# A perceiver layer on one Trainium2 core: the order of the first key matmuls and the first projection, 3 transfers for 24, and a later start of the ternary sums

## Chip, cores, metric

The kernel runs on one core of one Trainium2 chip. The metric is the device time of one execution in microseconds, as the median of several runs.

## What is computed

Eight sequences of 64 tokens (x, 512 wide) pass three residual blocks; ctx_2048 holds 1601 context rows for each sequence.

```python
# 1: cross attention over the context and self attention, quantised projections
ln_out = _ln(_layernorm(x), ln_w, ln_b)
q  = _ln(fp8_linear(ln_out, wq));  k = _ln(fp8_linear(ln_out, wk));  v = fp8_linear(ln_out, wv)
core = _gqa(q, k, v)                              # 16 heads in 8 groups, 128 wide
qx = _ln(fp8_linear(ln_out, wqx))
kx, vx = split(einsum('bsi,oi->bso', ctx_2048, w_kv_x))
kx = _ln(kx)
xout = _gqa(qx, kx, vx)                           # 1601 context rows
x = x + einsum(div_clamp_fp8(cat(core, xout)), wproj) * scales
# 2: token attention with a mask from a pairwise two-layer net, top 6 of 64 keys
x = x + sparse_attention(_layernorm(x))
# 3: feed forward, weights made ternary with a threshold of 0.7 of their mean magnitude
w1_q, w2_q = absmean_quant(w1), absmean_quant(w2)
x = x + einsum(gelu(einsum(_layernorm(x), w1_q) + b1), w2_q) + b2
```

## The kernel before

**Engines.** PE multiplies, ACT and DVE and POOL work elementwise, SP issues all transfers, each engine in its own order. Matrices that need more than one matmul pass of precision are split into a high part (a cast) and a low part (the remainder), and three products are summed: high x high, high x low, low x high.

**Cross attention.** Work is cut into 16 pieces (`Cross`, 8 sequences x 2 halves of the heads), each with 13 blocks of 128 context rows (`TT`; the last has 65). The main loop (L1156) has 227 slots; slot g does the keys of block g of the row of 208 blocks, and later stages of earlier blocks:
- `key_weights` (L491): loads the key weights of one half in four blocks of rows (`ic`), takes the mean off, casts `wkhi` on ACT (L501) and, for the first half, makes `wklo` on POOL (L502).
- `keys` (L542): loads a block of context (`cTr`), casts `cThi` on ACT (L549), makes `cTlo` on POOL (L550), 12 matmuls into `kx` (L555): four with `cThi` and `wkhi`, four with `cThi` and `wklo`, four with `cTlo` and `wkhi`. Then the squares (`ksq`, L560), a sum (`kxv`, L562), a power on POOL (`rqk`, L173) and the normalised `kn` on DVE (L564).
- `keys_t` (L567), one slot later: PE transposes `kn`, ACT and DVE make `kthi` and `ktlo`. Two buffers of `kt`, each holding a chunk of two or three blocks.
- `scores` (L580), two slots after a chunk's last keys: matmuls of `qxhi`, `qxlo` with `kthi`, `ktlo` (L598), which free the `kt` buffer. `queries` (L535) makes `qxhi` and `qxlo` on POOL before the first of them. Exponentials, transposes of the probabilities, context rows (`context`, L653) and the weighted sum (`weigh`, L678) follow 17 slots after the keys.
- `last_context` (L724), once, in slot 13: the last of the 1601 rows of all sequences is split into high and low; three rows (high, high, low) for each sequence are stored to `codd` in DRAM and loaded by `context` of the last block (L663).

**Background work.** Streams of generators are advanced in each slot: `bgA` 1.55 steps a slot and 4 from slot 142 (projections, self attention, output projection, token attention), `bgC` (the last pieces' end), `bgB` 0.4 steps a slot (`ternary`, L935). Their instructions are emitted at a lower priority and behind the slot's `pin` on DVE, that is behind the multiplication that makes `kn` (L564), by `issue_after` (L1242). `ternary` does for each of two weights 16 steps of a 256 KB load (`tern`) and a sum of magnitudes (L943, DVE), then 16 steps of a load, two DVE operations (L956, L958) and a store. The feed forward at the end reads the result, after slot 214. `tern` and the pairwise part of the token attention (`attn`, L760) share four buffers (`r2k`).

**The first projection** (`projection("qx", ..., first)`, L293) makes the first piece's queries: one step of five DVE operations that round the normalised tokens to fp8 (`b1y`, `xq`, L306 to L308), then four blocks of 256 columns: two weight loads (`ut`), four scalings on ACT (L325), eight matmuls (`pj`, L336), row statistics, and a transpose (`tr`, L372). In slot 0 all of it is emitted (`bgA.pump(ALL)`, L1184), behind the keys of block 0. The other tokens are normalised by `norms` (`token_norm`, L280: its result goes to DRAM as `lnTd` and is loaded again at L304), from slot 2, and are projected by the same function.

The instructions of an engine are not in the order of emission: the program is ordered when it is built, from priorities and simulated times (L1319).

Of the kernel before, what the change touches and what calls it, by code (L numbers as in the profile page):

```python
# [11 lines left out]
F32 = mybir.dt.float32  # L12
# [10 lines left out]
H = 512  # L23
NIC = 4
# [20 lines left out]
FAR = 3  # L45
PACE = 1.55, 4
LATER = 142
TERNARY_PACE, TERNARY_AT = 0.4, 8
HELD = "held"


# [6 lines left out]
def tile_perceiver(ctx: ExitStack, tc: tile.TileContext, t: dict):  # L58
    nc = tc.nc
    V, A, GP, PE = nc.vector, nc.scalar, nc.gpsimd, nc.tensor  # L60
# [3 lines left out]
    NB = NTOK // S  # L64
# [12 lines left out]
    def nm(s):  # L77
        uid[0] += 1
        return f"{s}_{uid[0]}"
# [4 lines left out]
    def sm(tag, k=1, dt=F32, bufs=None):  # L84
        kw = {} if bufs is None else {"bufs": bufs}
        return small.tile([P, k], dt, tag=tag, name=nm(tag), **kw)
# [5 lines left out]
    def mainp(tag="m"):  # L92
        return pm.tile([P, 512], F32, tag="m", name=nm(tag))

    def kxp(tag="kx"):


        if lane["late"] is not None:
            return lane["late"]
        return accp(tag) if lane["wide"] else mainp(tag)  # L100
# [28 lines left out]
    def load(dst, src):  # L129
        nc.sync.dma_start(dst, src)  # L130
        return dst
# [4 lines left out]
    def v3(ap, g):  # L136
        return ap.rearrange("p (g k) -> p g k", g=g)
# [4 lines left out]
    class Late:  # L142
# [13 lines left out]
        ps = staticmethod(lambda tag="b": kxp())  # L156
# [13 lines left out]
    def rsqrt(v, n, k, tag):  # L170

        y = sm(tag, k)
        GP.tensor_tensor(y[:n], v, mhalf[:n, :k], ALU.pow)  # L173
        return y[:n]
# [86 lines left out]
    def dtile(shape, dt, tag):  # L261
        return dram.tile(shape, dt, tag=tag, name=tag)
# [9 lines left out]
    wpd = [dtile([P, 2, H], F32, f"wpd{c}") for c in range(32)]  # L272
    clod = [dtile([SC, H], F32, f"clod{b}") for b in range(NB)]

    codd = [dtile([3, H], F32, f"codd{b}") for b in range(NB)]
    w1t = dtile([NIC, P, DFF], BF16, "w1t")
    w2t = dtile([NFC, P, H], BF16, "w2t")

# [170 lines left out]
    def cat_tile(tag):  # L449
        return ph.tile([P, 8, P], F32R, tag=tag, name=nm(tag), bufs=1)  # L450
# [69 lines left out]
    class Cross:  # L520
# [21 lines left out]
        def keys(self, tt):  # L542

            t0, n = TT[tt]
            raw = mp.tile([P, NIC, P], F32, tag="raw", name=nm("cTr"), bufs=3)
            paced[0] = nc.sync.dma_start(raw[:, :, :n], t["ctxT"][self.b].rearrange("(c p) k -> p c k", p=P)[:, :, t0:t0 + n])
            chi = mp.tile([P, NIC, P], F32R, tag="cThi", name=nm("cThi"), bufs=2)
            clo = mp.tile([P, NIC, P], F32R, tag="cTlo", name=nm("cTlo"), bufs=2)
            A.copy(chi[:, :, :n], raw[:, :, :n])  # L549
            GP.tensor_tensor(clo[:, :, :n], raw[:, :, :n], chi[:, :, :n].bitcast(F32), ALU.subtract)  # L550
            ps = kxp()
            k = 0
            for st, mv in ((chi, self.wk[0]), (chi, self.wk[1]), (clo, self.wk[0])):
                for ic in range(NIC):
                    PE.matmul(ps[:n], lhsT=st[:, ic, :n], rhs=mv[:, ic, :], start=k == 0, stop=k == 11)  # L555
                    k += 1
            kn = mp.tile([P, 512], F32, tag="kn", name=nm("kn"), bufs=3)
            sq = ksq
            v = sm("kxv", HG)
            A.activation(sq[:n, :, :D], v3(ps[:n], HG), AF.Square, scale=1.0 / math.sqrt(D))  # L560
            A.copy(kn[:n], ps[:n])
            V.tensor_reduce(v[:n], sq[:n], AX.X, ALU.add)  # L562
            r = rsqrt(v[:n], n, HG, "rqk")
            pin[0] = V.tensor_tensor(v3(kn[:n], HG), v3(kn[:n], HG), r.unsqueeze(2).to_broadcast([n, HG, D]), ALU.mult)  # L564
            self.kn[tt] = kn
# [158 lines left out]
    def last_context():  # L724
        raw = load(mp.tile([P, 512], F32, tag="raw", name=nm("cr"), bufs=3)[:NB], t["ctx"][:, SC - 1, :])
        hi = mp.tile([P, 512], F32R, tag="chi", name=nm("chi"), bufs=2)
        lo = mp.tile([P, 512], F32R, tag="clo", name=nm("clo"), bufs=2)
        A.copy(hi[:NB], raw)
        V.tensor_tensor(lo[:NB], raw, hi[:NB].bitcast(F32), ALU.subtract)
        for b in range(NB):  # L730
            for r, x in enumerate((hi, hi, lo)):
                nc.sync.dma_start(codd[b][r:r + 1], x[b:b + 1].bitcast(F32))

    ac = {}

# [403 lines left out]
    def norms(js):  # L1139
        for j in js:  # L1140
            token_norm(j)
            yield

    NT = len(TT)
    work = [Cross(b, half) for half in range(2) for b in range(NB)]
# [10 lines left out]
    for g in range(NA + LAG + 3):  # L1156
        nA, kA = divmod(g, NT)
        if g < NA and kA == 0:
            h = work[nA].half
            if h not in wk:  # L1160
                wk[h] = key_weights(h)
            work[nA].wk = wk[h]
        if g == LAG - 1:
            lane["wide"] = False
        if g == NA + 3:
            lane["late"] = mainp("late")
        e = g - LAG + 1
        if 0 <= e < NA:
            nE, kE = divmod(e, NT)
            w = work[nE]  # L1170
            if kE == CHUNKS[-1][0]:
                w.last_probs()
            w.context(kE)
            w.probs_t(kE)
            ci = CHUNK_OF[kE]
            if ci + 1 < NCH:

                with tc.issue_after(w.pin.ins):
                    w.exps(ci + 1, *((0, 2) if kE == CHUNKS[ci][0] else (2, 4)))
        if g == LAG - 4:  # L1180
            last_context()
        if g < NA:
            work[nA].keys(kA)
        if g == 0:  # L1184
            bgA.pump(ALL)
        if g == 2:
            bgA.add(norms(rest), projection("qx", range(4), rest), projection("qx", range(4, 8), range(NJ)),
                    projection("q", range(8), range(NJ)), projection("k", range(4), range(NJ)), projection("v", range(4), range(NJ)))
            bgA.add(*[self_attn(j) for j in range(NJ)])
            bgA.add(attn_consts())  # L1190
        if g == TERNARY_AT:
            bgB.add(ternary("ffn_w1", w1t), ternary("ffn_w2", w2t))
        if 0 <= g - 2 < NA:
            nS, kS = divmod(g - 2, NT)
            ci = CHUNK_OF[kS]
            w = work[nS]
            if kS == CHUNKS[ci][-1]:
                if ci == 0:
                    w.queries()
                w.scores(ci)  # L1200
                if ci == NCH - 1:
                    w.maxima()
                    w.exps(0, 0, 2)
        if 0 <= g - 3 < NA and (g - 3) % NT == NT - 1:
            work[(g - 3) // NT].exps(0, 2, 4)
        e = g - LAG
        if 1 <= e and e % NT == 0 and e // NT <= len(work):
            work[e // NT - 1].values()
        if 2 <= e and (e - 1) % NT == 0 and (e - 1) // NT <= len(work):
            w = work[(e - 1) // NT - 1]  # L1210
            key = (w.b // 2, w.half)
            j, odd = divmod(w.b, 2)
            split = w.half and j >= NJ - SPLIT
            if not odd:
                bgA.clear_front()
                if w.half:
                    bgA.pump(ALL)
                catq[key] = cat_tile("catx")
            w.cat(catq[key])
            if key != (NJ - 1, 1):  # L1220
                if not w.half:
                    if odd:
                        bgA.front.append(proj_part(j, 16, catq[key]))
                elif split or odd:
                    on = (odd * S, S) if split else (0, P)
                    bgA.add(finish(j, 24, catq[key], *on))
            elif not odd:
                bgC.add(proj_weights(24), finish(NJ - 1, 24, catq[key], 0, S, True, Late()))
            else:
                bgA.add(finish(NJ - 1, 24, catq[key], S, S, True))  # L1230
        if 0 <= e < NA:
            nE, kE = divmod(e, NT)
            work[nE].weigh(kE)
            if kE == NT - 1:
                work[nE].weighed()
        if 0 <= g - 1 < NA:
            nT, kT = divmod(g - 1, NT)
            work[nT].keys_t(kT)
        for bg, q in ((bgA, PACE[g >= LATER]), (bgC, PACE[1]), (bgB, TERNARY_PACE if g < NA + FFN_AT else 0)):
            n = int((g + 1) * q) - int(g * q)  # L1240

            with tc.issue_after(pin[0].ins), tc.issue_after(paced[0].ins) if bg is bgB else nullcontext(), tc.high_priority( -100):  # L1242
                bg.pump(n)
        if g == NA + FFN_AT:
            bgB.pump(ALL)
            if NJ > 2:
                bgB.add(ffn(list(range(NJ - 2)), 0))
                bgB.step()
# [74 lines left out]
```

## Time and profile before

| | |
|---|---|
| three runs, us | 1980.34, 1996.92, 1990.99 |
| median | 1990.99 us |
| span of the profiled execution, first to last instruction | 1990.0 us |
| mean granted clock of PE | 0.991 |
| instructions | 32306 |
| transfers | 352.02 MB, 177 GB/s on average |

The execution that was profiled has no other time than its span; it lies 1.0 us below the median of the three. The profile gives busy times of each engine (PE: matmuls, PEld: weight loads, DVE, ACT, POOL), the same in 40 slices of the span, the clock that PE was granted in tenths of full speed, and how busy the 16 transfer engines were. The chain of work that ended last is followed back from the last instruction; its largest shares:

```profile
PE 83%; DMA 7%; DVE 5%; issue 2%; ACT 1%; POOL 1%; SPq 0%; POOLq 0%; ACTq 0%; DVEq 0%
```

### The profile page before, as it was taken

The numbers are of one execution on the slowest core, as the hardware profiler recorded it, in microseconds if no ns is written. First come the engines' busy times: TensorE is split into PE (matmuls) and PEld (weight loads), VectorE is DVE, ScalarE is ACT, GpSimd is POOL, SyncE is SP. The second block draws the span as 40 slices with busy tenths as digits, with TensorE's granted clock in tenths as the row PEclk, the third lists the DMA queues.
The fourth block names the chain that finished last, engine by engine and source line by source line (L and its number), as shares of the span: only waits on it lengthen the run. The fifth ranks groups of instructions, "written<-read, shape, count | busy, mean of one in ns | idle before, by whom it ended". The sixth has DMA issues, their size and how long they took to land.

```text
span 1990.0 us, 32306 instructions
## 1 busy us (share of the span) xinstructions
PE 1923.4 (97%) x10709; PEld 1593.6 (80%) x10709; DVE 1377.2 (69%) x3423; ACT 1215.9 (61%) x2724; POOL 634.1 (32%) x600
## 2 busy tenths in 40 slices
PE   7899999999999999999999999999999999999998
PEld 5678888888888887887888788888877787886776
DVE  7768688677678676776775665756577665655665
ACT  6576667666676566655664545555675566566554
POOL 6343334333333333223332323222233333220132
PEclk9899999999999999999999999999999999999999
DMA  6345545466455654557776667656745543564425
GB/s 199 115 140 164 160 143 162 142 209 211 132 171 157 216 160 122 186 172 265 236 265 225 200 199 257 200 188 204 269 136 162 172 157 94 156 209 139 142 65 178
DMA packets 296503, 352.02 MB, mean 177 GB/s; under 512 B 30336, under 2 KB 191232, under 8 KB 296336
## 3 DMA queue, kind: packets, MB, share of 16 engines
q1 hardware_dynamic: 296336, 349.97, 55.5%
q8 instruction: 84, 1.38, 0.3%
q14 instruction: 83, 0.68, 0.1%
HBM read 283.94 MB, written 65.68 MB: 176 GB/s over the span
## 4 chain that ended last, share of the span: by engine, by line
PE 83%; DMA 7%; DVE 5%; issue 2%; ACT 1%; POOL 1%; SPq 0%; POOLq 0%; ACTq 0%; DVEq 0%
PE kx L555 26%; PE acc L693 8%; PE acc L694 8%; PE acc L695 8%; PE s L598 6%; PE pj L340 4%; PE pt L630 4%; PE kx L219 4%; DMA ws<-wpd 3%; PE xo L714 3%; PE pp L431 2%; PE p L822 1%; DMA wv<-in_wkv 1%; PE tr L372 1%; PE y L1073 1%
## 5 line engine op out<-in xcount | busy, mean ns | idle before, releaser
L550 POOL TENSOR_TENSOR cTlo<-cTr,cThi 128x512 fp32r<-128x512 f32 (+1 forms) x208 | 274.4, 1320 | 891.2 <-PE kx L555 618.1
L694 PE MATMUL acc<-plo,chi 128*128 128x512 f32 x768 | 310.3, 405 | 0.4 <-DVE plo L641 0.4
L695 PE MATMUL acc<-phi,clo 128*128 128x512 f32 x768 | 303.8, 397 | 0.0
L562 DVE TENSOR_REDUCE kxv<-ksq 128x4 f32<-128x516 f32 (+1 forms) x208 | 142.9, 687 | 223.0 <-ACT ksq L560 222.8
L173 POOL TENSOR_TENSOR rqk<-kxv,mhalf 128x4 f32<-128x4 f32 (+1 forms) x208 | 217.8, 1047 | 127.1 <-DVE kxv L562 109.5
L693 PE MATMUL acc<-phi,chi 128*128 128x512 f32 x768 | 246.7, 402 | 1.7 <-ACT chi L670 1.0
L555 PE MATMUL kx<-wkhi,cThi 128*128 128x512 f32 (+1 forms) x832 | 240.8, 411 | 7.0 <-ACT wkhi L501 2.3
L549 ACT CAST cThi<-cTr 128x512 fp32r<-128x512 f32 (+1 forms) x208 | 125.9, 606 | 182.1 <-PE kx L555 84.1
L555 PE MATMUL kx<-wklo,cThi 128*128 128x512 f32 (+1 forms) x832 | 230.4, 397 | 0.0
L555 PE MATMUL kx<-wkhi,cTlo 128*128 128x512 f32 (+1 forms) x832 | 229.4, 395 | 0.0
L577 ACT ACTIVATE kthi<-kx,cols 128x512 fp32r<-128x512 f32 (+1 forms) x208 | 140.8, 677 | 137.2 <-PE kx L219 135.6
L670 ACT CAST chi<-cr 128x512 fp32r<-128x512 f32 x192 | 119.1, 620 | 141.7 <-PE acc L694 130.5
L618 ACT ACTIVATE S<-S,cnm 128x256 f32<-128x256 f32 (+1 forms) x384 | 197.1, 522 | 7.0 <-DVE cnm L613 6.8
L578 DVE SCALAR_TENSOR_TENSOR ktlo<-kx,cols,kthi 128x512 fp32r<-128x512 f32 (+1 forms) x208 | 150.9, 726 | 60.7 <-ACT kthi L577 59.9
L555 PEld LDWEIGHTS kx<-wklo,cThi 128*128 128x128 f32 (+1 forms) x832 | 155.0, 187 | 41.2 <-issue 1.6
L555 PEld LDWEIGHTS kx<-wkhi,cTlo 128*128 128x128 f32 (+1 forms) x832 | 154.3, 186 | 41.3 <-issue 3.2
L555 PEld LDWEIGHTS kx<-wkhi,cThi 128*128 128x128 f32 (+1 forms) x832 | 147.5, 188 | 39.2 <-ACT wkhi L501 3.5
L564 DVE TENSOR_TENSOR kn<-kn,rqk 128x512 f32<-128x512 f32 (+1 forms) x208 | 149.4, 718 | 39.4 <-POOL rqk L173 36.3
L602 DVE CUSTOM_DVE_ANT_0 S<-s,zeros 128x256 f32<-128x256 f32 (+1 forms) x384 | 151.9, 429 | 33.1 <-PE s L598 32.2
L694 PEld LDWEIGHTS acc<-plo,chi 128*128 128x128 f32 x768 | 145.0, 189 | 26.4 <-issue 1.7
L693 PEld LDWEIGHTS acc<-phi,chi 128*128 128x128 f32 x768 | 139.9, 189 | 32.7 <-ACT chi L670 2.8
L695 PEld LDWEIGHTS acc<-phi,clo 128*128 128x128 f32 x768 | 144.6, 189 | 26.1 <-issue 1.6
(344 smaller groups left out, 3770.5 us busy)
## 6 DMA issues: line engine op xcount, KB each, us to landing
cTr<-in_ctxT SPq DMA_DIRECT2D x192, 256.0 KB
cr<-in_ctx SPq DMA_DIRECT2D x192, 256.0 KB
ws<-wpd SPq DMA_DIRECT2D x88, 512.0 KB
clod<-clo SPq DMA_DIRECT2D x96, 256.0 KB
clo<-clod SPq DMA_DIRECT2D x96, 256.0 KB
wv<-in_wkv SPq DMA_DIRECT2D x64, 256.0 KB
tern<-in_ffn_w SPq DMA_DIRECT2D x64, 256.0 KB
wpd<-ws SPq DMA_DIRECT2D x32, 512.0 KB
```

The lines of the kernel that those rows point to most:

```text
L173: GP.tensor_tensor(y[:n], v, mhalf[:n, :k], ALU.pow)
L550: GP.tensor_tensor(clo[:, :, :n], raw[:, :, :n], chi[:, :, :n].bitcast(F32), ALU.subtract)
L555: PE.matmul(ps[:n], lhsT=st[:, ic, :n], rhs=mv[:, ic, :], start=k == 0, stop=k == 11)
L562: V.tensor_reduce(v[:n], sq[:n], AX.X, ALU.add)
L564: pin[0] = V.tensor_tensor(v3(kn[:n], HG), v3(kn[:n], HG), r.unsqueeze(2).to_broadcast([n, HG, D]), ALU.mult)
L577: A.activation(hi[:, :, o], v3(pt, HG)[:, :, :n], AF.Copy, scale=hw["kx"])
L578: V.scalar_tensor_tensor(lo[:, :, o], v3(pt, HG)[:, :, :n], hw["kx"], hi[:, :, o].bitcast(F32), ALU.mult, ALU.subtract)
L602: V.tensor_tensor_reduce(sc[:, g, :cw], ps[:, :cw], zeros.to_broadcast([P, cw]), 1.0, -3.0e38, ALU.add, ALU.max, self.mx[:, g * NCH + ci:g ...
L618: A.activation(self.S[ci][:, g, :cw], self.S[ci][:, g, :cw], AF.Exp, bias=self.nmx[:, g:g + 1], accum_out=self.su[:, g * NCH + ci:g * NCH ...
L693: PE.matmul(self.U[ic], lhsT=chi[:n, s], rhs=phi[:n], start=tt == 0, stop=False)
L694: PE.matmul(self.U[ic], lhsT=chi[:n, s], rhs=plo[:n], start=False, stop=False)
L695: PE.matmul(self.U[ic], lhsT=clo[:n, s], rhs=phi[:n], start=False, stop=False)
```

## The change

Four edits. (1) For the first block of keys alone, the 12 matmuls go by block of weight rows, with the three products of a block together. (2) The rest of the first projection is emitted in slot 1, behind the second keys, and no longer in slot 0; its first step comes with the background work at the end of slot 0. (3) `codd` is one DRAM tensor of three rows for each of eight sequences, written by three transfers. (4) The ternary stream starts in slot 30 instead of 8.

```diff
-TERNARY_PACE, TERNARY_AT = 0.4, 8
+TERNARY_PACE, TERNARY_AT = 0.4, 30
...
-    codd = [dtile([3, H], F32, f"codd{b}") for b in range(NB)]
+    codd = dtile([NB, 3, H], F32, "codd")
...
-            k = 0
-            for st, mv in ((chi, self.wk[0]), (chi, self.wk[1]), (clo, self.wk[0])):
-                for ic in range(NIC):
-                    PE.matmul(ps[:n], lhsT=st[:, ic, :n], rhs=mv[:, ic, :], start=k == 0, stop=k == 11)
-                    k += 1
+            order = [(st, mv, ic) for st, mv in ((chi, self.wk[0]), (chi, self.wk[1]), (clo, self.wk[0])) for ic in range(NIC)]
+            if tt == 0 and self is work[0]:
+                order = [(st, mv, ic) for ic in range(NIC) for st, mv in ((chi, self.wk[0]), (clo, self.wk[0]), (chi, self.wk[1]))]
+            for k, (st, mv, ic) in enumerate(order):
+                PE.matmul(ps[:n], lhsT=st[:, ic, :n], rhs=mv[:, ic, :], start=k == 0, stop=k == 11)
...
-        for b in range(NB):
-            for r, x in enumerate((hi, hi, lo)):
-                nc.sync.dma_start(codd[b][r:r + 1], x[b:b + 1].bitcast(F32))
+        for r, x in enumerate((hi, hi, lo)):
+            nc.sync.dma_start(codd[:, r, :], x[:NB].bitcast(F32))
...
-        if g == 0:
+        if g == 1:
             bgA.pump(ALL)
```

## The prediction

> **What bounds the kernel now.** I read the totals and the 40 slices of the page first, then the list of who made PE (TensorE) wait, then the timeline of the first 130 us.
>
> ```profile
> PE 1923.4 (97%) x10709; PEld 1593.6 (80%) x10709; DVE 1377.2 (69%) x3423; ACT 1215.9 (61%) x2724; POOL 634.1 (32%) x600
> PE   7899999999999999999999999999999999999998
> ```
>
> PE is busy for 1923.4 of 1990.0 us: all idle time is 66.6 us. Only the ends of the slice line fall below 9. An edit that removes no matmul can win only from these 66.6 us and from matmuls that run at half pace. PE's waits up to 130 us:
>
> ```profile
> PE tr L219 <- DVE fa L201: 10.8, 1, 10.8
> PE pj L340 <- ACT ws L325: 4.6, 1, 4.6
> PE pt L630 <- ACT S L618: 2.4, 1, 2.4
> PE kx L555 <- ACT wkhi L501: 2.3, 2, 1.9
> PE kx L555 <- ACT cThi L549: 2.1, 1, 2.1
> ```
>
> With four smaller ones (1.7, 1.6, 1.2, 1.0) this makes 27.7 us; 10.8 of it is before the first transpose, whose load and row norm the change leaves alone. So 16.9 us of early idle time are open to it. The timeline of PE in the start:
>
> ```profile
> 15.84 0.80 PE L555 MATMUL kx<-wkhi,cThi 128*128 128x512 f32 x1 [1.91 <-ACT wkhi L501]
> 16.43 1.91 PE L555 MATMUL kx<-wklo,cThi 128*128 128x512 f32 x4
> 18.14 1.91 PE L555 MATMUL kx<-wkhi,cTlo 128*128 128x512 f32 x4
> 19.93 8.14 PE L336 MATMUL pj<-ws,xq 128*128 128x256 f32 x32
> 29.06 1.08 PE L555 MATMUL kx<-wklo,cThi 128*128 128x512 f32 x4
> ```
>
> Four key matmuls follow one another every 0.43 us at 16.4 and every 0.23 us at 29. Counts per microsecond put the step at 21.8 us (3 projection matmuls a microsecond before it, 6 after). The granted-clock column reads 1.00 there; it does read 0.50 at 68 to 72 us, after the stall at 62.9 to 67.5, with the same 0.43 us pace.
>
> **First keys by blocks of rows.** 12 matmuls stay 12. The old order needs all four blocks of the high weights (wkhi) before any low one: PE stands 1.91 us for the fourth block (cast at 15.17 on ACT), and 8 of the 12 matmuls are still to come at 16.43. In the new order, blocks 0 to 2 can be done by then: the context's low part was ready at 13.57 (POOL L550, 11.85+1.72), wklo block 2 at 15.24 (13.53+1.71), block 3 at 17.25 (15.86+1.39). After block 3's two matmuls on wkhi the last one starts at 17.25 and is done by 17.7, against 20.0 now: 2.3 us earlier. Two ACT scalings of the projection's weights (0.91 us at 14.37) that stand before the fourth cast now lose their place, which may give another 0.7. But what fills the freed time runs at the slow pace until about 21.8, so 2.3 us of it hold 2.3 x 0.23/0.43 = 1.2 us of later work. Bounds 1.2 and 2.3+0.7 = 3.0; I take 2.0, between the paces.
> In the Trainium skill, "TensorE: Matmul & The Clock Gate", Part 1, says that the array runs at half rate until a window of about 3.4 us was busy. By that rule a denser start could release the clock a little earlier, and the gain would go towards 3 us, the sum below from 4.5 to 5.5; the row above (busy from 15.84, fast at 21.8) needed some 6 us and does not settle it.
>
> **First projection behind the second keys.** 32 matmuls, 8 weight loads, 16 ACT scalings, four DVE chains: the same instructions, later. Emitted now in slot 0 in whole, it will give its first step (five DVE operations that make xq) at the end of slot 0, at low priority and behind the normalisation kn of the first keys (L564, done at 23.24 now, about 21 then, as its matmuls end 2.3 earlier); the rest follows the second keys. The five operations took 14.52 to 19.88 = 5.4 us beside POOL's weight splitting; the same forms elsewhere take 0.69+0.28+0.28+0.28+0.42+0.68 = 2.6. So xq is there at 23.6 to 26.4 instead of 19.9. PE does not stand: the second keys' high part is ready at 17.9, the low part at 19.34, the third's at 21.45. SP's transfer for the second keys (issued at 11.20, behind four loads of the projection's weights) may go earlier. Behind it: the projection ends 4 to 6.5 us later, and its chain of four transposes and the split into qxhi and qxlo with it. The split ends at 42.32 now and the first scores start at 46.27: 3.95 us of cover. Beyond it, the next key transposes need the kt buffers that these scores free; PE has one more block of keys (2.8 us) to pull ahead. A shift of 6.5 us less 3.95 is 2.55, under 2.8. Cost 0 to 2.5; I take 0.5, as the cover is nearly always enough.
>
> **Ternary sums from slot 30.** The pace of 0.4 a slot puts 9 steps between slots 8 and 30; they move behind. Each is a 256 KB load (0.50 us of SP) and a reduction of 0.68 us on DVE: 6.1 us of DVE until 250 us (9 rows there). Nothing waited for these reductions. The loads do meet the critical chain at one place:
>
> ```profile
> 49.82 0.33 SPq L290 DMA_DIRECT2D lnTd<-fb  x1
> 52.22 0.33 SPq L130 DMA_DIRECT2D ld<-lnTd  x1
> ...
> 54.01 0.32 SPq L290 DMA_DIRECT2D lnTd<-fb  x1
> 57.01 0.32 SPq L130 DMA_DIRECT2D ld<-lnTd  x1
> ...
> 58.30 0.49 SPq L130 DMA_DIRECT2D tern<-in_ffn_w  x1
> 58.89 0.38 SPq L290 DMA_DIRECT2D lnTd<-fb  x1
> 63.35 0.33 SPq L130 DMA_DIRECT2D ld<-lnTd  x1
> 63.77 0.39 SPq L130 DMA_DIRECT2D ld<-in_wqx  x1
> ```
>
> From storing lnTd to the load back it takes 2.4 and 3.0 us, but 4.5 when a ternary load goes in just ahead. SP holds in_wqx behind it, ACT's scaling of that waits, and PE stands 4.6 us. Without the ternary load the weights come up to 4.5-3.0 = 1.5 to 2.1 us earlier; a shorter stall also shortens the slow stretch (12 key matmuls at 0.43 instead of 0.23 = 2.4 us). But DVE is full from 55 to 65 us, with nothing ternary in it, and sets xq anyway. Bounds 0 and 2.1+2.4 = 4.5; I take 2.0.
> The other end: 64 steps end near slot 189 instead of 167, from 1530 to about 1530 x 189/167 = 1730 us. The 9 steps that come there are splits, 0.57+0.74 = 1.3 us of DVE each, 12 us over 200 us in which DVE is idle for 74 (200 less 126 busy, 1550 to 1750). Cover holds: 0. The weights that they write are read after slot 214. They share four r2k buffers with the pairwise part of the token attention; a wait there costs PE at most what it idles now in that stretch, 2.6 us.
>
> **Odd context rows in 3 transfers.**
>
> ```profile
> L732 SPq DMA_DIRECT2D codd<-chi x16: 232/250/455, 76.9 to 92.1; - x16
> L732 SPq DMA_DIRECT2D codd<-clo x8: 215/250/251, 78.3 to 92.4; - x8
> ```
>
> 21 issues of 0.25 us less: 5.3 us of SP. Only the five between 90.99 and 92.66 stand right before a context load that PE wants, and PE stands 2.1 us at 96.3 to 98.4 for its cast. But on ACT that cast stands behind a copy that waits for PE's own transposes (until 96.8), so the load alone would not move it. Bounds 0 and 2.1; I take 1.0.
> [...]
>
> **Sum.** 2.0 - 0.5 + 2.0 + 1.0 = 4.5 us. 1990.0 - 4.5 = 1985.5 for the span; the median of the three runs (1980.34, 1996.92, 1990.99) is 1.0 above the span: 1986.5.
>
> **Rivals.**
> 1. *The late projection delays the first scores* (slower). It decides once they start after 46.27+2.8 = 49.1 us. If DVE takes the five operations late and PE does the third and fourth keys first, the projection starts at 30 instead of 19.9: scores at 46.27+10-3.95 = 52.3, a stall of 3.2 us and 2.4 us of half pace behind it, and the later norms, which end in the 4.6 us stall, slip by as much: 5.6+5.6 less the gains of 4.5 = +6.7: 1998. For it: xq is now tied to kn; against: PE waited only 1.5 us between 20 and 57.
> 2. *All of it is hidden*: the 62.9 to 67.5 stall is DVE's, and takes up whatever the start gained: 1991.
> 3. *The whole early stretch closes*: 16.9 us of idle and 5.5 of half pace: 1968.6. Every wait would have to go; they have eight different causes.
> 4. *The order changes elsewhere.* The program's order on each engine is made from simulated times (L1319), so a moved step can shuffle later slots. Between 130 and 1850 us PE idles only some 24 us; 20 more would make 2011. Nothing in the profile says which way.
>
> **How the numbers follow.** Forecast 0.53, rival 1 0.22, rival 2 0.13, rival 3 0.04, rival 4 0.08. Three runs scatter from -11 to +6 us about their median, and 1% (20 us) is about what a measurement can tell from no change. Range 1974 to 1999: the forecast less that scatter, up to rival 1. Faster by over 1% takes rival 3 and luck: 0.05. Slower: rival 4: 0.08. Within: 0.87.
>
> **What will show it.** First keys done near 17.7; second keys before the first projection matmul, which starts at 24 to 26; first scores by 47; no ternary row before 230 us; storing lnTd to loading it at 3 us or less; PE idle before 130 us near 23. A stall of over 3 us ahead of the first scores, or over 35 us of idle between 130 and 1850, would make the forecast wrong.

## The result and the profile after

The changed kernel takes 2008.84 us (median of 6 runs, 2006.23 to 2013.36) against 1990.12 us for the kernel before in the same comparison. The ratio is 1.0086 with a 95% interval of 1.0064 to 1.0108: it is slower, by some 17 us. The execution that was profiled took 2009.42 us; its span is 2007.7, so 1.7 us lie around the span.

The totals and PE's slices of the changed kernel's page:

```profile
PE 1931.3 (96%) x10709; PEld 1600.2 (80%) x10709; DVE 1369.9 (68%) x3423; ACT 1213.4 (60%) x2724; POOL 634.8 (32%) x600
PE   6899999999999998999999999999999999999998
```

The same 10709 matmuls keep PE busy for 7.9 us more (1931.3 against 1923.4: more of them at the low clock), and PE idles 9.8 us more (76.4 against 66.6). The first slice falls from 7 to 6. PE's longest waits up to 140 us, in the list of who waited for whom (total, times, longest):

```profile
PE tr L219 <- DVE fa L201: 10.8, 1, 10.8
PE pj L336 <- DVE xq L308: 5.9, 1, 5.9
PE pj L340 <- ACT ws L325: 5.3, 1, 5.3
PE kx L219 <- DVE kn L564: 2.6, 2, 2.4
```

The second line is new: the first projection waits 5.9 us for xq. The two waits that the edits were thought to shorten differ: the one for `wkhi` is gone, the one for the projection's weights (`ws`) is 5.3 instead of 4.6. The timeline of PE in the start:

```profile
18.05 0.50 PE L556 MATMUL kx<-wklo,cThi 128*128 128x512 f32 x1
18.39 1.09 PE L556 MATMUL kx<-wkhi,cThi 128*128 128x512 f32 x4
19.32 1.09 PE L556 MATMUL kx<-wklo,cThi 128*128 128x512 f32 x4
20.24 1.07 PE L556 MATMUL kx<-wkhi,cTlo 128*128 128x512 f32 x4
27.19 9.49 PE L336 MATMUL pj<-ws,xq 128*128 128x256 f32 x32 [5.88 <-DVE xq L308]
```

The first keys are through at 18.5 (20.0 before), and the second keys run at once, at the fast pace of 0.23 us: both are done at 21.3, where the kernel before had done the first and 1.4 us of the projection. Up to here the change leads. Then PE has nothing: its next instruction is the projection, and PE does not step past it to the third keys, which start at 37.1 although POOL has made the low parts of the third and the fourth block by 23.95. The same stretch in windows (length, PE busy and matmuls, granted clock, transfer share, GB/s):

```profile
23.50:27.00 3.50, 0.00 (x0) 0.73 0.89 256
27.00:31.60 4.60, 4.41 (x10) 0.50 0.05 19
31.60:36.50 4.90, 4.90 (x23) 0.97 0.00 2
```

During the wait the clock was taken down (0.73 on average from 23.5 to 27, so 0.50 from about 25.1), and the first 10 projection matmuls ran at 0.50. The 32 took 9.49 us against 8.14 before. The wait's cause is on DVE:

```profile
21.07 1.75 DVE L564 TENSOR_TENSOR kn<-kn,rqk 128x512 f32<-128x512 f32 x1 [1.15 <-POOL rqk L173]
22.74 1.75 DVE L306 TENSOR_TENSOR b1y<-r2k,rin 128x512 bf16<-128x512 f32 x1
24.42 0.68 DVE L562 TENSOR_REDUCE kxv<-ksq 128x4 f32<-128x516 f32 x1
...
26.45 0.69 DVE L308 TENSOR_TENSOR xq<-b1y,b1k 128x512 f32<-128x512 bf16 x1
```

The step is six operations in the trace (L306, L207, L209, L211, L212, L308), not five. The first (`b1y`, L306) stands right behind `kn` of the first keys, and a sum of the second keys (`kxv`) comes in between. DVE was idle from 14.1 to 19.2 meanwhile, with b1y's input ready at 14.5. The last ends at 27.1, 7.2 us later than before. The first scores start at 51.0 instead of 46.3.

### The profile page after: what moved, and what is told of

It is laid out like the page before. It is cut to its first block, busy times and chain, and to the rows that moved or that the text cites. A ratio compares the mean times of both kernels' runs of the same rounds, so it can differ in the third digit from the quotient of the medians.

```text
span 2007.7 us, 32287 instructions
## 1 busy us (share of the span) xinstructions
PE 1931.3 (96%) x10709; PEld 1600.2 (80%) x10709; DVE 1369.9 (68%) x3423; ACT 1213.4 (60%) x2724; POOL 634.8 (32%) x600
## 4 chain that ended last, share of the span: by engine, by line
PE 84%; DMA 6%; DVE 4%; ACT 2%; issue 1%; POOL 1%; SPq 0%; POOLq 0%; DVEq 0%; ACTq 0%
PE kx L556 26%; PE acc L693 8%; PE acc L694 8%; PE acc L695 8%; PE s L598 6%; PE pj L340 4%; PE pt L630 4%; PE kx L219 4%; PE xo L714 3%; PE pp L431 3%; DMA ws<-wpd 2%; PE p L821 1%; DMA wv<-in_wkv 1%; PE po L485 1%; PE y L1072 1%
## 5 line engine op out<-in xcount | busy, mean ns | idle before, releaser
L694 PEld LDWEIGHTS acc<-plo,chi 128*128 128x128 f32 x768 | 145.0, 189 | 26.4 <-issue 1.7
```

The lines of the kernel that those rows point to most:

```text
L694: PE.matmul(self.U[ic], lhsT=chi[:n, s], rhs=plo[:n], start=False, stop=False)
```

## The experiments

Theory A: the tie of the projection's first step to `kn`, which the background loop sets (`issue_after` at the end of slot 0), makes PE wait and costs most of the loss. Rivals: the late ternary stream, or the order of the later slots that any edit shuffles. Each kernel is compared with the kernel before on the same chip.

| kernel | ratio to before | 95% interval |
|---|---|---|
| changed | 1.0086 | 1.0064 to 1.0108 |
| only_proj (edit 2) | 1.0045 | 1.0025 to 1.0065 |
| only_proj_free (edit 2, xq free) | 1.0009 | 0.9992 to 1.0025 |
| only_tern (edit 4) | 1.0032 | 1.0010 to 1.0054 |
| only_order (edit 1) | 0.9986 | 0.9972 to 1.0001 |
| order_again (edit 1, once more) | 0.9979 | 0.9962 to 0.9995 |
| only_codd (edit 3) | 1.0010 | 0.9996 to 1.0025 |
| all_but_proj | 1.0026 | 1.0010 to 1.0042 |
| all_but_tern | 1.0030 | 1.0016 to 1.0044 |
| all_free_xq | 1.0023 | 1.0007 to 1.0038 |
| all_no_edge | 1.0012 | 0.9994 to 1.0030 |
| free_tern8 (edits 1 to 3, xq free) | 1.0001 | 0.9984 to 1.0019 |
| order_free (edits 1 and 2, xq free) | 0.9984 | 0.9967 to 1.0000 |
| tern_pause | 1.0012 | 0.9992 to 1.0032 |
| tern_fast | 1.0000 | 0.9981 to 1.0019 |

**One edit undone.** From the changed kernel:

```diff
-        if g == 1:
+        if g == 0:
             bgA.pump(ALL)
```

> The changed kernel with the first projection back in slot 0 (edits 1, 3 and 4 stay). Theory A, the five operations that make xq, tied to kn of the first keys, cost the start some 5 us: PE's wait for xq (5.9 us) is gone, first scores near 45 instead of 51, and the time is about 5 us under the changed kernel's 2008.8, so near 2003. Rival B, the late ternary steps and the shuffled order made all of the loss, and the early loss is taken up later: 2008 again. Rival C, the projection alone made all of it: 1990 or less.

1.0026, that is 0.60% (12 us) under the changed kernel: more than the 5 us expected. It is still over 1, so the first projection alone is not all of the loss.

```diff
-TERNARY_PACE, TERNARY_AT = 0.4, 30
+TERNARY_PACE, TERNARY_AT = 0.4, 8
```

> The changed kernel with the ternary stream from slot 8 as before (edits 1 to 3 stay). Theory A: the start still loses 5 us and the rest, some 13 us, came with the ternary start: near 1995. Rival B1, the ternary start cost nothing and the rest is the shuffle of the order by edits 1 to 3: 2008. Rival B2, all of the loss is the ternary start: 1988 to 1991.

1.0030, or 6 us over, about what theory A gave it, and 0.56% under the changed kernel, with the wait for xq still there (6.2 us). So both edits count, and neither rival takes the whole.

**One edit alone.** From the kernel before, edit 2:

```diff
-        if g == 0:
+        if g == 1:
             bgA.pump(ALL)
```

> The kernel before with edit 2 alone (the rest of the first projection in slot 1, its first step at the end of slot 0). Theory A: PE waits 4 to 6 us for xq before the first projection matmul, and the time is 4 to 6 us over 1990, near 1995. Rival: the wait is taken up by slack behind it, 1990. Rival: it costs more than the start shows, 2000 or over, since the order of later slots changes.

1.0045, or 9 us (5 to 13 by the interval), at or over the upper end of theory A. Its trace has PE waiting 4.6 us for xq, a wait that the list of the kernel before does not have.

Edit 4 alone:

> The kernel before with edit 4 alone (ternary from slot 30). Theory A (the ternary start costs 10 us or more by what comes late, between 560 us and the end): 2000 to 2004, with the same start as before up to 45 us. Rival: the late steps are covered and the early ones are saved: 1986 to 1990.

1.0032, or 6 us, in the interval 2 to 11: less than theory A's 10 at the likeliest, and no saving on the whole. Where it saves and where it loses is taken up below.

Edit 1 alone, in two sets of runs:

> The kernel before with edit 1 alone (first keys by block of rows). By the start alone: first keys done at 18.4 instead of 20.0, gain 1 to 2 us, 1988 to 1989. Rival: the order of later slots moves, and the time with it, by up to 10 us to either side.

> The kernel before with edit 1 alone once more, in more rounds: -0.14% was measured with an interval that just took in zero. If the 2 us of the start come through, -0.05 to -0.25%; if not, 0.

0.9986 and 0.9979; the second interval leaves out 1. It gains some 3 to 4 us and is the only version here that is clearly faster than the kernel before (1985.77 against 1988.47 us). Its PE, in the timeline:

```profile
18.50 0.63 PE L556 MATMUL kx<-wklo,cThi 128*128 128x512 f32 x1
20.40 6.31 PE L336 MATMUL pj<-ws,xq 128*128 128x256 f32 x28 [1.27 <-DVE xq L308]
```

The projection waits 1.27 us, and 28 of its matmuls then go at 0.23 us each, where the kernel before started them at the slow pace, which lasted there until 21.8.

Edit 3 alone:

> The kernel before with edit 3 alone (3 transfers for 24). By the transfers alone: 5 us less of SP around 77 to 92 us, gain 0 to 2 us, 1988 to 1990. Rival: the order of later slots moves, and the time with it, by up to 10 us to either side.

1.0010: no gain, and no loss that the interval settles.

**xq free.** All four edits, but the first step emitted in slot 0 where it was:

```diff
+        if g == 0:
+            bgA.pump(1)
         if g == 1:
             bgA.pump(ALL)
...
-            n = int((g + 1) * q) - int(g * q)
+            n = int((g + 1) * q) - int(g * q) if g else 0
```

> All four edits, but the first step of the projection (xq) is emitted in slot 0 at ordinary priority and not behind kn; only the weights, matmuls and norms come behind the second keys. Theory A: xq is ready before 20 us, PE does not wait for it, first scores near 43 to 45, and the time is 5 to 8 us under the changed kernel, 2001 to 2004; with the shuffle undone by luck it could be under 1990. Rival: the wait for xq moves to the second keys' low part and nothing is gained: 2008.

1.0023: 0.63% (13 us) under the changed kernel, more than the 5 to 8 us expected, though the two intervals together reach down to 7. The same edit on edit 2 alone:

> The kernel before with edit 2 and xq emitted in slot 0 at ordinary priority, not behind kn. Theory A: no wait for xq, the start as fast as before or 1 us faster, 1988 to 1991; the difference to edit 2 alone is the price of the tie, 4 to 6 us. Rival: the move costs as much without the tie: 1995.

1.0009 against 1.0045 with the tie: the tie costs 0.36%, some 7 us (2 to 12 by the two intervals), with the other edits away. The traces agree: the first key matmul of block 2 starts at 36.1 to 37.7 us in the four executions with the tie, and at 28.5 to 30.4 in the five that have edit 2 with xq free, 7.6 us apart in the mean. Moving the rest of the projection costs nothing measurable. Taking only the edge away and leaving the low priority:

```diff
-            with tc.issue_after(pin[0].ins), tc.issue_after(paced[0].ins) if bg is bgB else nullcontext(), tc.high_priority( -100):
+            with tc.issue_after(pin[0].ins) if g else nullcontext(), tc.issue_after(paced[0].ins) if bg is bgB else nullcontext(), tc.high_priority( -100):
```

> The changed kernel with one thing taken away: in slot 0 the background step is no longer put behind kn on DVE; its low priority stays. Theory A (the tie to kn, not the priority nor the later emission, is what makes PE wait for xq): the projection matmuls start near 23 with a wait under 2 us, and the time is that of the kernel with xq free, 0.2 to 0.3% over the kernel before, 11 to 13 us under the changed one. Rival (low priority is enough to hold it): wait near 6 us, 0.9% over.

1.0012. On every engine this program has the same order of instructions as all_free_xq, so the two are one program measured twice (1.0023 and 1.0012), and the low priority held nothing. Its timeline of PE:

```profile
17.85 1.19 PE L556 MATMUL kx<-wkhi,cThi 128*128 128x512 f32 x4
18.88 1.07 PE L556 MATMUL kx<-wklo,cThi 128*128 128x512 f32 x4
19.79 3.61 PE L336 MATMUL pj<-ws,xq 128*128 128x256 f32 x16
```

and of DVE:

```profile
17.69 0.69 DVE L308 TENSOR_TENSOR xq<-b1y,b1k 128x512 f32<-128x512 bf16 x1
```

With xq done at 18.4, the projection starts at 19.8 without a wait, at the fast pace: even earlier than the 23 expected. That the tie makes PE wait is shown by taking this one edge away. Its price in the whole change, 13 to 15 us, is more than the 7 us of the start; where the rest would be lost is not shown, and the intervals reach down to 7 and 9 us.

**The ternary stream.** Two ways to part its early from its late slots, from the kernel before: resting in slots 100 to 121 (same early slots, late end), and from slot 30 at a higher pace (early slots empty, the same end).

```diff
-(bgB, TERNARY_PACE if g < NA + FFN_AT else 0)
+(bgB, TERNARY_PACE if g < NA + FFN_AT and not 100 <= g < 122 else 0)
```

> The kernel before with the ternary stream from slot 8, but resting in slots 100 to 121, so that its last step is in slot 187 and not 167; nothing is taken from the early slots. Theory L (the late end of the ternary stream costs what edit 4 alone cost, 0.32%): some 6 us over the kernel before. Rival E (it is the early slots, or the order made there): within 2 us of it.

```diff
-TERNARY_PACE, TERNARY_AT = 0.4, 8
+TERNARY_PACE, TERNARY_AT = 0.466, 30
```

> The kernel before with the ternary stream from slot 30 at a pace of 0.466 instead of 0.4, so that its last step is in slot 165. Theory L: no cost, within 2 us of the kernel before. Rival E (the early slots without the stream, or the order made there): some 6 us over it.

1.0012 and 1.0000, each with 0.2% to either side. An empty early stretch costs nothing in tern_fast, which speaks against rival E; a late end costs 2 us at the likeliest, but its interval (up to 1.0032) still takes in the 6 us of edit 4. So these two ratios do not settle theory L; the traces of all kernels, taken together below, place the loss.

**Whether the parts make the whole.**

> All four edits with xq free of kn and the ternary stream from slot 8. If the tie and the ternary start are all of the loss: at or under the kernel before, -0.3 to 0%. Rival (edits 1 to 3 cost by the order that they make in later slots): 0.2% over or more.

1.0001: without the tie and with the ternary stream where it was, edits 1 to 3 cost nothing. The tie and the ternary start are therefore all of the 0.86%, to within the 0.2% of the interval. Alone, the four edits measured 0.45% (edit 2 with the tie), 0.32% (edit 4), 0.10% (edit 3) and -0.18% (edit 1, mean of two): 0.69% in sum, inside the interval of the whole (0.64 to 1.08%).

> The kernel before with edits 1 and 2 alone and xq free of kn (ternary from slot 8, 24 transfers). By the start: first keys 2 us earlier and no wait for xq: 0.1 to 0.4% under the kernel before. Rival: the gain of the start is taken up by later stalls: within 0.1%.

0.9984, the interval up to 1.0000: beside edit 1 alone (0.9979) the freed projection adds nothing that can be seen.

**Second profiles.**

> The kernel before once more, for a second profile: how far two executions of one program drift apart along the way. If the drift against the first profile stays under 1 us up to 500 us and reaches some 3 to 5 us behind, offsets of that size late in a single profile say nothing of an edit.

> The changed kernel once more, for a second profile: the loss of 5 us by 50 us must be there again (the wait of 5.9 us for xq and half pace behind it). If the other 12 us of its first profile are from the program's order, they are at the same places; if they are chance, at others.

From the traces, the start of the first key matmul of a block of keys, in us:

| block | before | before_again | changed | after_again |
|---|---|---|---|---|
| 2 | 31.5 | 30.5 | 37.1 | 37.7 |
| 48 | 385.7 | 388.4 | 391.1 | 387.0 |
| 88 | 730.3 | 740.0 | 739.3 | 733.4 |
| 168 | 1444.9 | 1446.4 | 1452.7 | 1448.4 |
| 206 | 1769.3 | 1771.2 | 1784.4 | 1778.2 |

The wait for xq is the same in the changed kernel's second execution:

```profile
27.21 10.05 PE L336 MATMUL pj<-ws,xq 128*128 128x256 f32 x32 [6.21 <-DVE xq L308]
```

Behind block 2, two executions of one program part by up to 9.7 us in this table and come closer again. Only the early loss is readable in a single trace; the ternary loss, of 6 us, is not.

In all traces together it is. Ten profiled executions have the stream from slot 8 at a pace of 0.4 (before, before_again, all_but_tern, only_proj, only_order, order_again, only_codd, only_proj_free, order_free, free_tern8), six have edit 4 (changed, after_again, all_but_proj, all_free_xq, all_no_edge, only_tern). The table gives the time between the first key matmuls of two blocks, as mean and range in us; block 2 lies behind the wait for xq, and block 64 is where the lead of edit 4 is widest.

| stretch | ten without edit 4 | six with edit 4 | tern_pause | tern_fast |
|---|---|---|---|---|
| block 2 to 64 | 494.4 (490.3 to 501.1) | 487.5 (484.8 to 490.2) | 493.0 | 491.3 |
| block 64 to 206 | 1243.2 (1237.3 to 1249.3) | 1254.7 (1250.0 to 1261.2) | 1245.8 | 1245.1 |
| in it, PE waits that DVE ended | 5.2 (3.8 to 7.1) | 12.0 (10.6 to 13.6) | 6.9 | 10.6 |
| the same, from block 160 to 206 | 0.7 (0.7 to 0.9) | 3.6 (2.9 to 4.0) | 4.0 | 5.2 |
| block 206 to the end | 223.4 (220.7 to 226.8) | 224.3 (221.6 to 226.3) | 220.9 | 222.7 |

In the first four rows the ranges of the ten and the six do not meet. Edit 4 saves some 7 us up to block 64 and loses some 11.5 us between there and block 206: about 5 us in all, close to what its ratio said (0.32% alone, and 0.22% between all_free_xq and free_tern8). Of the loss, 6.8 us are longer waits of PE for DVE, the engine that the late steps run on, and tern_pause, which only ends late, has these waits from block 160 on. That the waits are the whole price is not shown: tern_fast has as many (10.6) without the longer stretch, in its one trace.

## Why the prediction was wrong

The forecast was 1986.5 us, 0.2% faster; it is 0.9% slower, and outside the range of 1974 to 1999. Of the signs that it named, the stall of over 3 us ahead of the first scores came (5.9 us); PE's waits between 130 and 1850 us, 22.8 before, came to 29.0, under its 35. By the prediction's steps:

- *First projection behind the second keys, cost 0 to 2.5, taken 0.5.* This step failed. That xq would be tied to `kn` was seen, and its time (23.6 to 26.4) came out at 27.1, 0.7 us beyond. What followed, "PE does not stand", was wrong. The prediction let PE fill the time with the third keys, whose inputs were ready at 21.45; but in PE's order the projection stands ahead of the third keys, and PE stood from 21.3 to 27.2 rather than take them, with their inputs there from 22.3 on (`cTlo`). The 3.95 us before the first scores cover a late projection, not idle PE time: the wait came whole, 5.9 us, with 1.35 us of slower matmuls behind it (9.49 less 8.14). Freeing xq is worth 0.36% with edit 2 alone (7 us) and 0.63 to 0.74% in the whole change (0.86 less 0.23 and less 0.12).
- *Rival 1, the late projection.* The right mechanism, by the wrong road: first scores at 51.0, beyond its point of 49.1, but through a wait for xq and not through third and fourth keys done first. Its price (6.7 us, to 1998) was too low: it took off 4.5 us of gains, 2.0 of them from the ternary start, which lost some 6 us instead.
- *Ternary from slot 30, gain 2.0 taken from 0 to 4.5, and cover of the late steps at 0.* Wrong in sign: 0.32% slower alone. The early half was right, and some 7 us came of it up to block 64 (second profiles above). From storing `lnTd` to loading it, the three took 3.5, 2.6 and 3.6 us in the changed kernel, as its SP queue shows:

```profile
54.50 0.52 SPq L290 DMA_DIRECT2D lnTd<-fb  x1
58.01 0.33 SPq L130 DMA_DIRECT2D ld<-lnTd  x1
...
62.55 0.32 SPq L290 DMA_DIRECT2D lnTd<-fb  x1
65.10 0.32 SPq L130 DMA_DIRECT2D ld<-lnTd  x1
...
66.35 0.32 SPq L290 DMA_DIRECT2D lnTd<-fb  x1
69.92 0.32 SPq L130 DMA_DIRECT2D ld<-lnTd  x1
```

  The third, 4.5 before, took 2.5 to 3.7 us in the six executions with edit 4 and 3.9 to 4.5 in the ten without. The stall behind it scatters more: 3.9 to 5.3 us (mean 4.5) against 4.6 to 8.2 (mean 6.4), so 1.9 us shorter in the mean, near the 2.0 taken. What failed is "Cover holds: 0". It was argued from the sum of DVE's idle time; the runs show a stretch of 11.5 us more between blocks 64 and 206, with 6.8 us more of PE waiting for DVE.
- *First keys by blocks, gain 2.0 from 1.2 to 3.0.* Right, and small: 2.8 us (0.14%) and 4.2 us (0.21%, over the bounds, though its interval reaches down to 1) in the two measurements of edit 1. Its working was off in two places, in opposite directions. The first keys ended at 18.5 and not at 17.7, since eleven matmuls at 0.43 us each followed from 13.62, when the first low part was there. And the bounds were built on a slow pace until 21.8, where the denser start had the fast pace at 18.4. The Trainium skill, "TensorE: Matmul & The Clock Gate", Part 1, says that one busy window of about 3.4 us lifts the clock. From the first matmul without a gap to the fast pace it took 4.8 us here (13.62 to 18.39) and 6.0 in the row of before (15.84 to 21.8): both are over that window, and neither contradicts it.
- *Odd rows, gain 1.0 from 0 to 2.1.* Within its bounds at 0: 1.0010 (0.9996 to 1.0025). The 2.1 us wait for the cast is gone from the changed kernel's list, and nothing at the end follows from it.
- *Rival 4, the order elsewhere.* Not needed for edits 1 to 3: with xq free, free_tern8 has another order of PE's instructions than the kernel before in over 200 places, most of the way through, and takes the same time. For the late ternary steps, the new order is not parted from the steps themselves.

## What to carry to other kernels

When a step is moved into a scheduled background stream, look at what that stream adds to it (a priority, an edge behind an instruction of the slot), and follow the edge to the engine that runs in order: what stands next in the program there is what will wait, whatever else is ready. A cover is only a cover if its instructions stand ahead of the waiting one in the same queue. Price a wait of PE with the matmuls at the lower clock behind it. And idle time of an engine, added up over a stretch, is not cover for work that is moved there: DVE had 74 us of it in 200, and PE waited for DVE more all the same.

## What the hardware showed

In the four executions with the wait for xq, the clock came down 2.5 to 5.2 us after PE's last matmul (21.3 to 25.1 in the changed kernel). A shorter wait could do it too: in the kernel before, PE waited 0.4 and 1.5 us between 769.8 and 772.3, and the clock read 0.50 from 772.9 to 776.3. In the traces here every stretch at 0.50 is 3.4, 6.8 or 10.2 us long, save the last, which the end of the trace cuts off. Such stretches add up to 38.1 and 50.8 us in two executions of the kernel before, 59.5 and 48.3 us in two of the changed one. Two executions of one program differ by up to 9.7 us in the middle and by 0.4% in time.
